# Layer 0's attention scores on column halves, with its last turns and layer 1's first norm in another order

## The chip, the cores and the metric

The kernel runs on one core of one Trainium2 chip. The metric is the device time of one execution in microseconds; a smaller time is better. Engines are named as in the profile: PE is TensorE (PEld its weight loads), DVE is VectorE, ACT is ScalarE, POOL is GpSimd, and SP is the engine that issues most DMAs.

## The reference, cut to what matters

Two transformer layers on x of 2 batches x 512 tokens x 512 features, all in float32. Each layer is attention and then a feed-forward, both on a normalised x that is scaled and shifted by columns of `mod`, and both added to x times a gate:

```
mod = silu(c) @ wmod                       # six rows of 512 per batch: shift, scale, gate, twice
h   = layernorm(x) * (1 + ca) + sa
x   = x + ga * attention(h)
h   = layernorm(x) * (1 + cb) + sb
x   = x + gb * ffn(h)
```

Layer 0's attention has 8 key heads, each with 4 query heads of size 128. A query at position i sees only the keys j with i - 128 < j <= i:

```
scores = einsum('bqhgd,bshd->bhgqs', qg, k) * sm_scale
allowed = (j <= i) & (j > i - SLIDING_WINDOW)          # SLIDING_WINDOW = 128
attn   = softmax(where(allowed, scores, neg))
out    = attn @ v ;  return out @ wo
```

So 128 consecutive queries see at most 256 consecutive keys: the first 64 of them see only the first 192 of these, and the last 64 only the last 192. Layer 0's feed-forward is a dense product with a bias and a weighted sum of 16 low-rank updates. Layer 1's attention has 128 heads with latent keys, and takes most of the time; the change does not touch it.

## The kernel before

**Layer 0's attention** (`attention0`, L662). A unit is one key head and one batch: 16 units, batch 0 and batch 1 of a head in turn. Each unit has four turns, one for each block of 128 queries (`qb`). The loop over n (L812) runs one turn at a time, and its order is written out by hand for PE, ACT, DVE and POOL (`manual_schedule`): each of these engines works through its instructions in the order of the program. In turn n the loop issues

1. `scores` of turn n: 4 products (one a head) into the PSUM tile `s`; DVE adds the mask `band` (L743) and takes the negated maximum (L749); ACT takes four exponentials (L753). The keys are 256 wide, in the first block of a unit (`qb` 0) 128 wide;
2. keys, values or queries of the next unit (`roped`, L685, and `values`, L707);
3. `normalised` of turn n: DVE's reciprocal (L762), POOL's product (L763);
4. `turned` of turn n-1: transposes on PE (L772), copied from PSUM to `pT` by ACT and DVE (L774);
5. `output` of turn n-2: the product with wo (L797), DVE's product with the gate (`ya`, L805), POOL's addition to x (L806);
6. `mix` of turn n-1: the product with the values (L783), copied to `oT` by DVE (L790);
7. what stands in `aside` (the modulation products, `mod_rows`, L101, in early turns) and in `steps[n]`.

The tile `s` has one buffer, taken anew in each turn. Products leave PE through PSUM tiles of the tag `mm`, four buffers in rotation (`pmm`), shared by queries, values, mix, output, and all of `finale`.

**The end of layer 0** (`finale`, L568). The last unit's turns are n = 60 to 63, with no queries left to compute; n = 64 and 65 finish mix and output. `finale` gives `steps`, what is done after turn n, and `rest`, what is done after the loop. In them stand layer 0's second norm `n0` (statistics by DVE, L160; `rows`: a square root on ACT, L168, a reciprocal and four scaled tiles `xn` on DVE, L173; `turn`: transposes on PE, L182, that leave as `hT` through ACT for even and DVE for odd blocks of features, L192 and L190) and the feed-forward `Ffn0`: `bias` (the bias times the gate), `add_bias` (POOL, L246), `low` (L251, the low-rank inputs of a batch) and `tile` (L264 and L268, one block of 128 tokens). Batch 0's attention is complete some turns before batch 1's, so its norm and its `low` are done beside the last turns.

**The start of layer 1** (`attention1`). Under a second hand-written order come the loads of the down-projections (L946) and of `Wq_up` and `Wk_up` (L950), whose halves ACT casts (L953, L954) and DVE subtracts (L955). Then, for each batch, `normalised` (the last function of `adaln_kernel`) and three down-projections (L971), whose results leave through DVE (L981) into a pool `psm1a` of three PSUM buffers. For batch 0 `normalised` transposes layer 1's first norm, `norm1`, and takes batch 1's statistics and rows; for batch 1 it transposes and spreads the gates (L140).

**The start of the kernel.** `silu_c` (L76) loads c for each layer on POOL's queue; SP's queue loads the modulation weights, x, the tables and layer 0's weights.

Of the kernel before, what the change touches and what calls it, by code (L numbers as in the profile page):

```python
# [10 lines left out]
F32 = mybir.dt.float32  # L11
# [7 lines left out]
P = 128  # L19
# [4 lines left out]
EPS = 1e-5  # L24

NKV, GRP, HD, WIN = 8, 4, 128, 128

NH, HD1, LAT, ROPE = 128, 4, 64, 64
SCALE1 = float(1.0 / np.sqrt(np.float32(HD1 + ROPE)))
# [13 lines left out]
def adaln_kernel(ctx: ExitStack, tc: tile.TileContext, A: dict, out: bass.AP):  # L43
# [161 lines left out]
    class Ffn0:  # L205
# [6 lines left out]
        def loads(self):  # L212
            self.wT = self.wmp.tile([P, KC, D], F32, tag="wmod", name="wT0", bufs=2)
            nc.sync.dma_start(out=self.wT, in_=A["L0_ffn_WT"].rearrange("(kc p) o -> p kc o", p=P))

            self.ab = self.wmp.tile([P, KC, D], F32, tag="wmod", name="abT0", bufs=2)
            nc.sync.dma_start(
                out=self.ab[:, :, : 2 * P], in_=A["L0_ffn_AT"].rearrange("(kc p) e -> p kc e", p=P)
            )
            for j in range(2):  # L220
                nc.sync.dma_start(
                    out=self.ab[:, 2 * j : 2 * j + 2, 2 * P :],
                    in_=A["L0_ffn_BT"][j * P : (j + 1) * P, :].rearrange("p (h o) -> p h o", h=2),
                )
            co = self.mid.tile([P, 2, 2], F32, tag="co", name="co0")
            for i, n in enumerate(("L0_ffn_coeffs", "L0_ffn_scales")):
                for j in range(2):
                    src = A[n][j * 8 : (j + 1) * 8].unsqueeze(1).to_broadcast([8, R]).unsqueeze(2)
                    nc.sync.dma_start(out=co[:, i, j : j + 1], in_=src)
            self.wrow = self.mid.tile([P, 2], F32, tag="wrow", name="wrow0")  # L230
            nc.vector.tensor_mul(self.wrow, co[:, 0, :], co[:, 1, :])

        def bias(self):

            row = self.ap.tile([P, D], F32, tag="t1", name="biasrow0")
            nc.sync.dma_start(out=row, in_=A["L0_ffn_bias"].unsqueeze(0).to_broadcast([P, D]))
            self.gb = [
                self.ap.tile([P, D], F32, tag="t2", name=f"gb{b}") for b in range(B)
            ]
            for b in range(B):  # L240
                nc.gpsimd.tensor_mul(self.gb[b], row, self.gate[b])
            self.xa = self.ap.tile([P, GRP, S], F32, tag="qT", name="xa")

        def add_bias(self, b):
# [280 lines left out]
    with ExitStack() as c01:  # L525
# [7 lines left out]
        with ExitStack() as c00:  # L533
# [34 lines left out]
            def finale(ap, pool):  # L568
# [44 lines left out]

        def normalised(b, pool):

            norm1.turn(b, range(KC), pool)
            if b == 0:
                for t in range(TB, NT):
                    norm1.stats(t)
                norm1.rows(1)  # L620
            else:
                spread_gates(1, (2, 5), grow[1], pool, gate)


# [3 lines left out]
def weights0(tc, A, ctx):  # L628
# [10 lines left out]
    def tables():  # L639

        rope = tab.tile([P, 4, S], F32, tag="rope", name="rope")
        nc.sync.dma_start(out=rope, in_=A["c_rope"])
        band = tab.tile([P, 2 * P], F32, tag="band", name="band")
        nc.sync.dma_start(out=band, in_=A["c_band"])
        return rope, band

# [15 lines left out]
def attention0(tc, small, hT, xs, ga, ident, tabs, groups, load_group, aside, finale):  # L662
# [11 lines left out]
    with ExitStack() as ctx:  # L674
# [4 lines left out]
        kTs, vs, qTs, oTs, sps, pes, pTs = ({} for _ in range(7))  # L679

        def roped(dst, wcols, b, tables, name):

# [47 lines left out]

        def scores(u, qb):

            k0, nk = window(qb)
            sp = pss.tile([P, GRP, 2 * P], F32, tag="s", name=f"s{u}_{qb}")
            for hh in range(GRP):
                nc.tensor.matmul(  # L736
                    sp[:, hh, :nk],
                    lhsT=qTs[u][:, hh, qb * P : (qb + 1) * P],
                    rhs=kTs[u][:, k0 * P : k0 * P + nk],
                    start=True,  # L740
                    stop=True,
                )
            nc.vector.tensor_add(  # L743
                sp[:, :, :nk],
                sp[:, :, :nk],
                band[:, 2 * P - nk :].unsqueeze(1).to_broadcast([P, GRP, nk]),
            )
            nm = small.tile([P, GRP], F32, tag="nm", name=f"nm{u}_{qb}")
            nc.vector.tensor_reduce(nm, sp[:, :, :nk], AX.X, ALU.max, negate=True)  # L749
            pe = ap.tile([P, GRP, 2 * P], F32, tag="p", name=f"p{u}_{qb}", bufs=3)  # L750
            rs = small.tile([P, GRP], F32, tag="rs", name=f"rs{u}_{qb}")
            for hh in range(GRP):
                nc.scalar.activation(  # L753
                    pe[:, hh, :nk], sp[:, hh, :nk], AF.Exp,
                    bias=nm[:, hh : hh + 1], accum_out=rs[:, hh : hh + 1],
                )
            pes[u, qb] = pe, rs
# [48 lines left out]
            nc.gpsimd.tensor_add(xs[t], xs[t], y)  # L806

        aside = aside(pmm)
        steps, rest = finale(ap, pmm)
        aside.pop(0)()  # L810
        with tc.manual_schedule(engines=FOUR):
            for n in range(-TB, NU * TB + 2):  # L812
# [725 lines left out]
def _constants():  # L1538
# [12 lines left out]
    band = np.where((j > i) & (j <= i + WIN), 0.0, -1e30).astype(np.float32)  # L1551

    r = np.arange(P) % 16
    lowq = (r // 4 % 2 == 1).astype(np.float32)
# [70 lines left out]
```

## Time and profile before

| | us |
|---|---|
| median of 3 runs | 2522.49 (2519.63 to 2522.56) |
| the profiled execution's own time | 2519.66 |
| its span, from first to last instruction | 2517.9 |
| PE busy in the span | 2453.7 (97%) |
| DVE busy | 1684.2 (67%) |
| ACT busy | 1401.9 (56%) |
| POOL busy | 1571.9 (62%) |

Layer 0's attention takes the span up to about 866 us, its feed-forward up to about 916, layer 1 the rest. A line of a timeline reads: start in us from the span's start, duration in us, engine, line of the kernel, operation, what is written <- what is read, shape in the array and of the operands, how many records; in brackets the idle time before it and what ended it. A product of f32 operands shows as two PE records. The durations of PE's records overlap, so the distance from start to start tells what one costs.

### The profile page before, as it was taken

What the parts mean: (1) busy time and instruction counts of PE and PEld (TensorE: products, weight loads), DVE (VectorE), ACT (ScalarE), POOL (GpSimd) and SP (SyncE); (2) the same over time, 40 slices, a digit from 0 to 9 for tenths busy, and PEclk for the clock granted to TensorE, in tenths of its full rate; (3) what the DMA queues carried; (4) which work ended last, traced back from release to release, by engine and by line L of the source; (5) the groups of instructions that cost most, each with busy time, mean ns of one, the idle gap of its engine ahead of it and who ended that gap; (6) DMA issues with size and microseconds to landing.
All of it is one profiled execution on the core that took longest, in us unless ns stands there. A gap on an engine that the chain in (4) does not pass through costs nothing.

```text
span 2517.9 us, 28439 instructions
## 1 busy us (share of the span) xinstructions
PE 2453.7 (97%) x10252; PEld 1146.2 (46%) x10252; DVE 1684.2 (67%) x2309; ACT 1401.9 (56%) x2086; POOL 1571.9 (62%) x1521
## 2 busy tenths in 40 slices
PE   8999999999999899999999999999999999999877
PEld 3555555555555444444443444444344444444333
DVE  4445555555555435787778777778778877788764
ACT  2212112121221215888888788888888878888650
POOL 1333333333334323888888888888888888888643
PEclk9999999999999999999999999999999999999978
DMA  6211101001000100000000000000100000110000
GB/s 240 88 49 60 42 5 38 26 20 40 17 1 7 29 15 26 26 26 26 26 26 17 29 27 26 26 18 26 30 26 26 18 25 26 30 29 21 17 9 34
DMA packets 68697, 81.32 MB, mean 32 GB/s; under 512 B 6989, under 2 KB 49772, under 8 KB 68428
## 3 DMA queue, kind: packets, MB, share of 16 engines
q1 hardware_dynamic: 68348, 79.35, 10.1%
q8 instruction: 81, 1.33, 0.2%
q14 instruction: 60, 0.49, 0.1%
q0 software_dynamic: 208, 0.16, 0.0%
HBM read 77.40 MB, written 2.10 MB: 32 GB/s over the span
## 4 chain that ended last, share of the span: by engine, by line
PE 95%; DVE 3%; ACT 1%; DMA 0%; issue 0%; POOL 0%; SPq 0%; DVEq 0%; ACTq 0%; POOLq 0%
PE s L1081 19%; PE psq L1014 18%; PE acc L1236 10%; PE ps_q L685 9%; PE pw L797 8%; PE s L1090 5%; PE s L736 4%; PE po L783 4%; PE psv L707 2%; PE ps_k L685 2%; PE pt L772 2%; PE psu L1033 2%; PE psm L1160 2%; PE psw L1292 1%; PE psf L499 1%; PE psf L264 1%
## 5 line engine op out<-in xcount | busy, mean ns | idle before, releaser
L1187 POOL TENSOR_TENSOR ss<-ss,row 128x512 f32<-128x512 f32 x504 | 634.5, 1287 | 42.8 <-ACT row L1172 42.8
L1100 ACT COPY ss<-s 128x1024 f32<-128x1024 f32 x512 | 505.4, 1015 | 179.2 <-PE s L1090 130.5
L1081 PE MATMUL s<-q,ckr 64*128 64x512 f32 x2048 | 554.5, 612 | 10.7 <-ACT ss L1100 10.7
L1190 ACT ACTIVATE ss<-ss 128x1024 f32<-128x1024 f32 x512 | 525.2, 1070 | 5.6 <-DVE ss L1402 4.5
L1014 PE MATMUL psq<-hT,wqr 128*128 128x512 f32 x1024 | 466.7, 598 | 0.0
L1090 PE MATMUL s<-qm,c 64*128 64x512 f32 x1024 | 419.7, 795 | 0.4 <-DVE c L1051 0.4
L753 ACT ACTIVATE p<-s,nm 128x256 f32<-128x256 f32 (+1 forms) x256 | 110.9, 445 | 489.6 <-DVE nm L749 480.8
L1107 DVE TENSOR_TENSOR mx<-s,mx 128x1024 f32<-128x1024 f32 x256 | 306.6, 1218 | 41.2 <-PE s L1090 40.1
L695 POOL TENSOR_TENSOR qT<-t_q,t_q 128x512 f32<-128x512 f32 x64 | 81.2, 1269 | 402.6 <-DVE t_q L694 402.6
L1181 POOL TENSOR_TENSOR ss<-ss,rowe 128x512 f32<-128x512 f32 x252 | 317.9, 1285 | 0.0
L1014 PEld LDWEIGHTS psq<-hT,wqr 128*128 128x128 f32 x1024 | 189.0, 189 | 242.3 <-issue 211.7
L1081 PEld LDWEIGHTS s<-q,ckr 64*128 64x128 f32 x2048 | 184.1, 186 | 215.8 <-ACT ss L1100 97.3
L1236 PE MATMUL acc<-ss,vp 128*32 128x512 f32 x2048 | 266.9, 614 | 0.0
L1107 DVE TENSOR_TENSOR mx<-s,ss 128x1024 f32<-128x1024 f32 x128 | 156.7, 1224 | 117.1 <-ACT row L1172 79.7
L797 PE MATMUL pw<-wo,oT 128*128 128x512 f32 x512 | 230.3, 592 | 0.0
L685 PE MATMUL ps_q<-hT,wq 128*128 128x512 f32 x512 | 230.1, 592 | 0.0
L1112 DVE STREAM_TRANSPOSE mx<-mx 128x1024 f32<-128x1024 f32 x128 | 158.6, 1239 | 2.3
L1118 DVE TENSOR_REDUCE m<-mx 128x32 f32<-128x1024 f32 x128 | 156.1, 1219 | 4.4
L1090 PEld LDWEIGHTS s<-qm,c 64*128 64x128 f32 x1024 | 104.6, 187 | 118.8 <-issue 114.6
L1150 POOL TENSOR_TENSOR st<-mh,own_block 128x512 fp32r<-128x512 f32 x64 | 67.0, 1047 | 142.9 <-DVE mh L1146 142.9
L1183 DVE TENSOR_TENSOR ss<-ss,psm 128x512 f32<-128x512 f32 x252 | 155.7, 679 | 0.0
L685 PEld LDWEIGHTS ps_q<-hT,wq 128*128 128x128 f32 x512 | 96.0, 190 | 102.3 <-issue 100.6
(208 smaller groups left out, 3089.5 us busy)
## 6 DMA issues: line engine op xcount, KB each, us to landing
wqr<-in_L_attn_Wq_rope_pairs SPq DMA_DIRECT2D x64, 512.0 KB
wmod<-in_L_wmod SPq DMA_DIRECT2D x12, 1024.0 KB
wq<-in_L_attn_wq SPq DMA_DIRECT2D x8, 1024.0 KB
wo<-in_L_attn_wo SPq DMA_DIRECT2D x8, 1024.0 KB
x<-in_L_attn_x SPq DMA_DIRECT2D x8, 256.0 KB
wk<-in_L_attn_wk SPq DMA_DIRECT2D x8, 256.0 KB
wv<-in_L_attn_wv SPq DMA_DIRECT2D x8, 256.0 KB
out<-yf SPq DMA_DIRECT2D x8, 256.0 KB
```

The costliest lines, as they stand in the source:

```text
L685: nc.tensor.matmul(ps, lhsT=wcols(kc), rhs=hT[b][:, kc, :], start=(kc == 0), stop=(kc == KC - 1))
L797: nc.tensor.matmul(ps, lhsT=oTs[u][:, hh, i * P : (i + 1) * P], rhs=groups[g]["o"][:, hh, :], start=(hh == 0), stop=(hh == GRP - 1),)
L1014: nc.tensor.matmul(ps, lhsT=wqs[t][:, kc, pair * P : (pair + 1) * P], rhs=hT[b][:, kc, :], start=(kc == 0), stop=(kc == KC - 1),)
L1081: nc.tensor.matmul(out[:, j, :], lhsT=whole[b]["kr"][r, bass.ts(i, P)], rhs=qs[t, p][r, :], start=True, stop=False,)
L1090: nc.tensor.matmul(out[:, j, :], lhsT=qkc[t // 2, 1][r, bass.ts(i, P)], rhs=qm[t, p][r, :], start=False, stop=True,)
L1100: nc.scalar.copy(ss[t, i, p], hold["s", t, i, p])
L1107: nc.vector.tensor_max(mx[t, p], hold["s", t, i, p], before)
L1112: nc.vector.transpose(m, m)
L1181: nc.gpsimd.tensor_sub(s, s, hold["r", t, 2])
L1187: nc.gpsimd.tensor_sub(s, s, hold["r", t, 2 * p + 1])
L1190: nc.scalar.activation(ss[t, i, p], ss[t, i, p], AF.Exp)
L1236: nc.tensor.matmul(accs[g, b][32 * h : 32 * (h + 1), :], lhsT=vps[t][:, kb, h, :], rhs=ss[t, kb, h // 2][:, h % 2, :], start=(s == 0 and k ...
```

## The change

- **Scores.** For `qb` above 0 each head's product is two: queries 0 to 63 of the block against keys 0 to 191 into output rows 0 to 63, queries 64 to 127 against keys 64 to 255 into rows 64 to 127. One PSUM tile `sp` is taken once and filled with -1e30 by DVE; the corners that no product writes keep that value, and `band` is 0 there. In block 0 the 128 keys now stand in the right half of the tile, with a third block of columns in `band` for them.
- **c first.** The loads of c go to SP's queue, ahead of the modulation weights.
- **The bias row** of feed-forward 0 gets a buffer of its own and is loaded with the other constants of the feed-forward (turn 20), not in turn 60.
- **The end of layer 0.** Statistics and rows of `n0`'s batch 0 come one turn later; a new list `filling` puts its four transposes, `add_bias` and the first `low` between output and mix of turn 63, and the second `low` between output and mix of turn 64; the last statistic and `tile(2)` change places in `rest`.
- **Layer 1's first norm.** `norm1`'s statistics and rows of batch 0 come between tiles 4 to 6 of the feed-forward, and its transposes between tiles 6 and 7; `normalised(0)` only takes batch 1's statistics and rows.

The diff, without the changes that only rename or copy:

```diff
@@ silu_c
-        nc.gpsimd.dma_start(out=c, in_=A[f"L{L}_cT"])
+        nc.sync.dma_start(out=c, in_=A[f"L{L}_cT"])
@@ Ffn0.loads, Ffn0.bias
+            self.row = self.mid.tile([P, D], F32, tag="biasrow", name="biasrow0")
+            nc.sync.dma_start(out=self.row, in_=A["L0_ffn_bias"].unsqueeze(0).to_broadcast([P, D]))
...
-            row = self.ap.tile([P, D], F32, tag="t1", name="biasrow0")
-            nc.sync.dma_start(out=row, in_=A["L0_ffn_bias"].unsqueeze(0).to_broadcast([P, D]))
@@ finale
                 for i in range(TB):
-                    steps[end + 2 + i] = [lambda i=i: n0.stats(i)]
-                    steps[end + 6 + i] = [lambda i=i: n0.stats(TB + i)]
+                    steps[end + 3 + i] = [lambda i=i: n0.stats(i)]
+                for i in range(TB - 1):
+                    steps.setdefault(end + 7 + i, []).append(lambda i=i: n0.stats(TB + i))
                 steps[end + 4].insert(0, f.bias)
-                steps[end + 5].append(lambda: n0.rows(0))
-                steps[end + 6].insert(0, lambda: n0.turn(0, (0, 1), pool))
-                steps[end + 7] = [
-                    lambda: n0.turn(0, (2, 3), pool), lambda: f.add_bias(0), lambda: f.low(0, 0)
-                ] + steps[end + 7]
-                steps[end + 8].insert(0, lambda: f.low(0, 1))
+                steps[end + 6].insert(1, lambda: n0.rows(0))
+
+                filling = {
+                    end + 7: [
+                        lambda: n0.turn(0, (0, 1), pool), lambda: n0.turn(0, (2, 3), pool),
+                        lambda: f.add_bias(0), lambda: f.low(0, 0),
+                    ],
+                    end + 8: [lambda: f.low(0, 1)],
+                }
                 rest = [
+                    lambda: n0.stats(NT - 1),
                     lambda: n0.rows(1),
                     lambda: f.tile(0),
                     lambda: f.tile(1),
+                    lambda: f.tile(2),
                     lambda: n0.turn(1, range(KC), pool),
                     lambda: f.add_bias(1),
-                    lambda: f.tile(2),
                     lambda: f.tile(3),
                     lambda: f.low(1, 0),
                     lambda: f.low(1, 1),
                 ]
-                for t in range(TB, NT):
-                    rest.append(lambda t=t: f.tile(t))
-                    rest.append(lambda t=t: norm1.stats(t - TB))
-                rest.append(lambda: norm1.rows(0))
-                return steps, rest
+                for i in range(TB):
+                    if i < 2:
+                        rest.append(lambda i=i: norm1.stats(i))
+                    rest.append(lambda i=i: f.tile(TB + i))
+                    if i == 1:
+                        rest.append(lambda: norm1.stats(2))
+                        rest.append(lambda: norm1.stats(3))
+                        rest.append(lambda: norm1.rows(0))
+                    if i == 2:
+                        rest.append(lambda: norm1.turn(0, range(KC), pool))
+                return steps, filling, rest
@@ normalised
-            norm1.turn(b, range(KC), pool)
-            if b == 0:
+            if b:
+                norm1.turn(b, range(KC), pool)
+            else:
@@ attention0
+        sp = pss.tile([P, GRP, 2 * P], F32, tag="s", name="scores")
+        nc.vector.memset(sp, NEVER)
@@ scores
             k0, nk = window(qb)
-            sp = pss.tile([P, GRP, 2 * P], F32, tag="s", name=f"s{u}_{qb}")
-            for hh in range(GRP):
+            o = 2 * P - nk
+            for hh in range(GRP) if qb == 0 else ():
                 nc.tensor.matmul(
-                    sp[:, hh, :nk],
-                    lhsT=qTs[u][:, hh, qb * P : (qb + 1) * P],
-                    rhs=kTs[u][:, k0 * P : k0 * P + nk],
+                    sp[:, hh, o:],
+                    lhsT=qTs[u][:, hh, :P],
+                    rhs=kTs[u][:, :P],
                     start=True,
                     stop=True,
                 )
+            for hh in range(GRP) if qb else ():
+                for h in range(2):
+                    lo, hi = h * H2, 2 * P - (1 - h) * H2
+                    nc.tensor.matmul(
+                        sp[h * H2 : (h + 1) * H2, hh, lo:hi],
+                        lhsT=qTs[u][:, hh, qb * P + h * H2 : qb * P + (h + 1) * H2],
+                        rhs=kTs[u][:, k0 * P + lo : k0 * P + hi],
+                        start=True,
+                        stop=True,
+                    )
             nc.vector.tensor_add(
-                sp[:, :, :nk],
-                sp[:, :, :nk],
-                band[:, 2 * P - nk :].unsqueeze(1).to_broadcast([P, GRP, nk]),
+                sp[:, :, o:],
+                sp[:, :, o:],
+                band[:, 0 if qb else 2 * P :][:, :nk].unsqueeze(1).to_broadcast([P, GRP, nk]),
             )
@@ the loop of attention0
                 if 0 <= n - 2:
                     output(*last)
+                for f in filling.get(n, ()):
+                    f()
                 if 0 <= n - 1 < NU * TB:
                     mix(*before)
@@ _constants
+    band = np.concatenate([band, band[:, P:]], axis=1)
+    band[:H2, 2 * P - H2 : 2 * P] = 0.0
+    band[H2:, :H2] = 0.0
```

More of the change, by code (lines that the diff above doesn't have):

```diff
@@ L26 @@
 NKV, GRP, HD, WIN = 8, 4, 128, 128
+H2 = P // 2
+NEVER = -1e30
 NH, HD1, LAT, ROPE = 128, 4, 64, 64
@@ L240, in bias @@
             for b in range(B):
-                nc.gpsimd.tensor_mul(self.gb[b], row, self.gate[b])
+                nc.gpsimd.tensor_mul(self.gb[b], self.row, self.gate[b])
             self.xa = self.ap.tile([P, GRP, S], F32, tag="qT", name="xa")
@@ L620, in normalised @@
                 norm1.rows(1)
-            else:
+            if b:
                 spread_gates(1, (2, 5), grow[1], pool, gate)
@@ L642, in tables @@
         nc.sync.dma_start(out=rope, in_=A["c_rope"])
-        band = tab.tile([P, 2 * P], F32, tag="band", name="band")
+        band = tab.tile([P, 3 * P], F32, tag="band", name="band")
         nc.sync.dma_start(out=band, in_=A["c_band"])
@@ L678, in attention0 @@
         pmm = ctx.enter_context(tc.tile_pool(name="psm0", bufs=4, space=PSUM, reuse_waits="tile"))
-        kTs, vs, qTs, oTs, sps, pes, pTs = ({} for _ in range(7))
+        kTs, vs, qTs, oTs, pes, pTs = ({} for _ in range(6))
+        sp = pss.tile([P, GRP, 2 * P], F32, tag="s", name="scores")
+        nc.vector.memset(sp, NEVER)
         def roped(dst, wcols, b, tables, name):
@@ L742, in scores @@
                 )
+            for hh in range(GRP) if qb else ():
[8 more added lines that the diff above has]
+                    )
             nc.vector.tensor_add(
-                sp[:, :, :nk],
-                sp[:, :, :nk],
-                band[:, 2 * P - nk :].unsqueeze(1).to_broadcast([P, GRP, nk]),
+                sp[:, :, o:],
+                sp[:, :, o:],
+                band[:, 0 if qb else 2 * P :][:, :nk].unsqueeze(1).to_broadcast([P, GRP, nk]),
             )
             nm = small.tile([P, GRP], F32, tag="nm", name=f"nm{u}_{qb}")
-            nc.vector.tensor_reduce(nm, sp[:, :, :nk], AX.X, ALU.max, negate=True)
+            nc.vector.tensor_reduce(nm, sp[:, :, o:], AX.X, ALU.max, negate=True)
             pe = ap.tile([P, GRP, 2 * P], F32, tag="p", name=f"p{u}_{qb}", bufs=3)
@@ L753, in scores @@
                 nc.scalar.activation(
-                    pe[:, hh, :nk], sp[:, hh, :nk], AF.Exp,
+                    pe[:, hh, :nk], sp[:, hh, o:], AF.Exp,
                     bias=nm[:, hh : hh + 1], accum_out=rs[:, hh : hh + 1],
@@ L808, in attention0 @@
         aside = aside(pmm)
-        steps, rest = finale(ap, pmm)
+        steps, filling, rest = finale(ap, pmm)
         aside.pop(0)()
@@ L1550, in _constants @@
     i, j = np.arange(P)[:, None], np.arange(2 * P)[None, :]
-    band = np.where((j > i) & (j <= i + WIN), 0.0, -1e30).astype(np.float32)
+    band = np.where((j > i) & (j <= i + WIN), 0.0, NEVER).astype(np.float32)
+    band = np.concatenate([band, band[:, P:]], axis=1)
+    band[:H2, 2 * P - H2 : 2 * P] = 0.0
+    band[H2:, :H2] = 0.0
     r = np.arange(P) % 16
```

## The prediction

> **What bounds the kernel now.** I read the chain that ended last, then the groups by line, then the stretches that the change touches as timelines. The chain's shares by engine:
>
> ```profile
> PE 95%; DVE 3%; ACT 1%; DMA 0%; issue 0%; POOL 0%; SPq 0%; DVEq 0%; ACTq 0%; POOLq 0%
> ```
>
> TensorE (PE) is the path. In the stage table it is busy for 747.3 of the 748 us between 60 and 808 us (layer 0's attention), for 50.5 of 58 between 808 and 866 (its end), and for 31.2 of 34 between 916 and 950 (the start of layer 1). So in attention an edit counts only by PE time; at the two seams by the PE gaps.
>
> **Part 1, scores on column halves.** PE timeline, one score step (L736) with its neighbours, 128*128 in the array throughout:
>
> ```profile
> 324.03 1.88 PE L783 MATMUL po<-pT,v 128*128 128x512 f32 x4
> 325.75 1.89 PE L736 MATMUL s<-kT,qT 128*128 128x256 f32 x8
> 327.47 3.73 PE L707 MATMUL psv<-wv,hT 128*128 128x128 f32 x32
> ```
>
> Read the starts: four 512-column records take 1.72 us, 0.429 each; eight 256-column ones 1.726, 0.216 each (four heads, two records for each f32 product). That is 0.8 ns a column and 2.5 ns more; 192 columns give 0.1625. Entering and leaving cost nothing. The new step issues 16 records of 64 output rows by 192 columns, half on rows 0-63 of the output, half on 64-127. Do two such halves run together, and is the change of shape free? No 64-column record exists here. The nearest row is the modulation product (L101), two neighbouring groups of 32:
>
> ```profile
> 113.10 1.88 PE L783 MATMUL po<-pT,v 128*128 128x512 f32 x4
> 114.91 3.63 PE L101 MATMUL psr<-wmod,sc 128*32 128x512 f32 x16
> 118.47 1.99 PE L736 MATMUL s<-kT,qT 128*128 128x256 f32 x8
> 120.30 0.94 PE L707 MATMUL psv<-wv,hT 128*128 128x128 f32 x7
> ```
>
> 16 records of 512 columns last about 8x0.429 = 3.43, so pairs do overlap fully. But L783 is through at 113.10+4x0.429 = 114.82, and 114.82 to 120.30 is 5.48, against 3.43+1.73 = 5.16 of streaming: 0.32 is lost by going in and out. Single records split it: on entry 0.092 before the first weight load starts and 0.026 for that load; on leaving 0.098 and 0.106. The Trainium skill, "TensorEngine Tiling (Array Packing)", Key Properties, has the rule that speaks against this change: going from one tiling mode to another drains the engine. Its "TensorE: Matmul & The Clock Gate", LDWEIGHTS, prices a load at columns/1.2 ns; the trace's 26 (32 columns) and 106 ns (128) agree, and 64 columns, which no row has, come to an estimated 53. So a new wide step is 8x0.1625 = 1.300 + 0.092+0.053 + 0.098+0.107 = 1.65, not 1.30: **-0.077 a step, 48 wide steps (16 units x 3): -3.7 us**. Without the drain rule it would be -0.426x48 = -20.5. Bounds: -20.5 (no price for the change of shape) and +59 (halves one after the other: 16x0.1625+0.35 = 2.95 a step). I take -3.7, since L101 measures both. DVE, ACT and POOL do the same work on the same shapes. The one-off fill of the score tile (128x1024 on DVE, nearest row the 1.23 us band addition) falls behind layer 0's first norm, where PE streams K and Q from 25 us on without waiting for DVE; uncovered it costs 1.2.
>
> **Part 2, the start.** The two loads of c leave POOL's queue and go ahead of the modulation weights on SP. The first products do wait for c (7.77 us), but their second half is released by
>
> ```profile
> 8.84 0.18 PEld L101 LDWEIGHTS psr<-wmod,sc 128*32 128x32 f32 x3 [0.89 <-DMA wmod<-in_L_wmod]
> ```
>
> so c early gains nothing. SP's issues here take 0.45 to 0.50 each, so wmod and x queue up to 0.9 later; between 0 and +0.9, as the DMA engines are full from 3 us on, I take **+0.6**. ffn 0's bias row moves to SP's issues at 40 us, long before use.
>
> **Part 3, the end of layer 0** (loop turns 60 to 65: no queries are left to cover the softmax). The costliest wait now is 5.47 us of PE in turn 62:
>
> ```profile
> 834.78 3.78 PE L783 MATMUL po<-pT,v 128*128 128x512 f32 x4 [5.47 <-ACT pT L774]
> ...
> 862.47 3.60 PE L797 MATMUL pw<-wo,oT 128*128 128x512 f32 x8
> ```
>
> DVE and ACT say why: the norm's rows (4 xn, 1.92 us, after a statistic that waits 1.12 for POOL) stand before the band addition, and the square root costs ACT a table load before the exponentials.
>
> ```profile
> 828.44 1.23 DVE L743 TENSOR_TENSOR s<-s,band 128x1024 f32<-128x1024 f32 x1
> 831.02 1.28 ACT L753 ACT_TABLE_LOAD   x1 [4.66 <-DVE nm L749]
> 834.13 0.60 ACT L774 COPY pT<-pt 128x512 f32<-128x512 f32 x1
> 834.28 0.18 DVE L762 RECIPROCAL rs<-rs 128x4 f32<-128x4 f32 x1 [3.36 <-ACT p L753]
> 834.96 0.68 DVE L805 TENSOR_TENSOR ya<-pw,g 128x512 f32<-128x512 f32 x1
> ```
>
> From band addition to pT copy's end is 6.3, to ya's end 7.2. The change moves this block one turn later and puts four transposes and the first `low` between output and mix. On the old clock the new order runs so. Turn 62: add at 824.9, no table load, mix at 829.9, a wait of 0.9. Then DVE: oT copy to 832.5, stats and rows to 835.85 (old: 825.12 to 828.44), band addition there, ya done at 843.05. PE in turn 63: scores, transposes, output to 837.6, three of the four new transposes to 838.9; the fourth needs the `mm` buffer (four in rotation) of the same turn's output, held by ya until 843.05. So what is moved in as filling waits for the same DVE queue: **the stall goes, but 4.2 us come back one turn later**. Then `low` to 847.0, mix to 848.7. Turn 64 goes through output and the second `low` to 856.5 and mix to 858.3; output 63 now follows its mix at once and waits 0.95 for the oT copy (that `low` used to hide it): end 862.65, old 862.47+3.43 = 865.90, **-3.2**. The clock takes part of it. The granted clock fell after these windows (columns: length, PE busy, PEld, DVE, ACT, POOL, clock, DMA):
>
> ```profile
> 829.50:832.80 3.30, 0.00 (x0) 0.00 (x0) 1.39 (x2) 1.76 (x4) 0.00 (x0) 1.00 0.00 0
> 914.80:918.20 3.40, 1.08 (x3) 0.19 (x1) 1.77 (x5) 0.30 (x1) 1.65 (x3) 1.00 0.82 212
> ```
>
> and stayed at a half for 6.8 us each time. "TensorE: Matmul & The Clock Gate", Part 1, has it fall after one idle window of about 3.4 us; here 1.08 of 3.40 busy sufficed. Of 4.2 idle us, one 3.4-window catches over 2.3 in nearly every phase, so it falls again. By the page's rule alone, a full window, it would mostly not, and I would leave out the next term: some 3 us of work at half speed, +1.6. **Sum -1.6**; ends -3.2 and 0.
>
> **Part 4, layer 1's first norm.** Today its batch 0 is transposed after the last feed-forward tile:
>
> ```profile
> 918.70 4.75 PE L182 MATMUL pst<-ident,xn 128*128 128x128 f32 x16 [2.82 <-DVE xn L173]
> 923.25 4.55 PE L971 MATMUL pscq<-hT,L_attn_Wq_down 128*128 128x512 f32 x8
> 938.70 3.70 PE L971 MATMUL pscq<-hT,L_attn_Wq_down 128*128 128x512 f32 x8
> ```
>
> Call U the end of the last tile's streaming (915.72). Batch 1's L971 starts at U+22.98. The new order puts the 16 transposes (1.75, as at 876.2) between tiles 6 and 7: rows come from DVE while tile 6 (5.15 us) streams, so nothing waits, and batch 0's L971 can start at U and end at U+10.3. But DVE then works through the two `up` differences (L955), which wait for Wq_up's load and ACT's casts, four statistics and batch 1's rows before it empties the first L971 buffer (the old run: 924.22 to 929.91, 5.7 us). L955 ends at 922.2 now (U+6.5), of which about 1.5 goes with the xn work ahead of it and with Wk_rope's issues, likely free sooner as the wider band shifts the feed-forward weights by 512 B: U+5. So the first emptying starts at U+10.7, the others 2 and 4 us later, and with three buffers batch 1's four transposes wait 1.1, 1.5 and 1.6: done at U+16.3, gate rows, L971 at U+18.6. Gain 22.98-18.6-1.75 = 2.6; without the shift 1.7. These waits make another nearly empty window; transposes there did not restore the clock before (918.2 to 921.6). I take +1.8: **-0.8**, ends -2.6 and +1.
>
> **Sum.** -3.7+0.6-1.6-0.8 = **-5.5 us**. The profiled execution took 2519.66 (span 2517.9 and 1.8 around it), which gives 2514.2. The median of three is 2522.49, 2.8 above it; two of three runs lie there. Taken off the median: **2517.0**. A measurement here tells about 0.2% (5.0 us) from no change.
>
> **Rivals.** (a) **The seams return nothing**: part 3's and 4's waits and clock falls cost all they save (DVE is late by the same work, wherever it stands). For: the dependence of every filler on DVE. Against: 865.90 against 862.65. -3.7+0.6+0.5: about 2520, chance 0.22. (b) **More than I grant**: the clock stays up at both seams (-8.9, 2513.5; chance 0.07), for which the free phase of the windows speaks, or the change of shape is free (-22, 2500; 0.04), against which L101 speaks. (c) **Slower**: the weight loads are not hidden behind passes as short as 0.16. Eight loads of 53 ns show in each wide step: 2.07 in place of 1.73, +0.35x48 = 16.7, less 1.8: about 2537. Against: L707 hides 128-column loads behind 128-column passes at 0.11 a record. For: there all of the array is one group. It decides from 1.87 us a step, (1.8+5.0)/48 above today's. Chance 0.12.
>
> **Chances and range.** My forecast 0.55, itself 2512 to 2522: its middle lies near the 0.2% bound, so 0.33 faster and 0.22 the same. With (a) 0.20 same and 0.02 slower, (b) 0.11 faster, (c) 0.12 slower: faster 0.44, same 0.42, slower 0.14. The range 2509 to 2526 leaves out the free change of shape and most of (c).
>
> **What would show it.** Wide L736 steps 1.65 us start to start of the neighbours (1.30: drain wrong; 2.07 or 2.95: loads or halves exposed). In turn 62 a PE wait below 1.5; in turn 63 one near 4 us ahead of the fourth transpose, released by DVE ya; a wait before output 63. No wait before layer 1's first L971, but waits for `fq`, `ckv`, `ckr` ahead of batch 1's transposes. A wrong price of the shape change moves the sum most: 0.1 us is 4.8.

## The result and the profile after

The changed kernel takes **2512.44 us** (median of 5 runs, 2509.96 to 2514.69); the kernel before, run beside it, 2522.49 (median of 5, 2517.6 to 2522.95). The ratio is **0.9967, 95% interval 0.9954 to 0.998**: faster by 0.33%. The forecast was 2517.0 (2509 to 2526): sign and range held, and the gain in the median, 10.05, is nearly twice the 5.5 of the sum. The excess is less sure than it looks: the means differ by 8.7, and in the 19 and 22 runs beside the experiments the kernel before has medians of 2519.6 and 2520.53, against which the gain is 7 to 8. The profiled execution took 2511.97, its span fell from 2517.9 to 2510.2.

How the -7.7 of the span is spread over the stages shows that the sum came near for the wrong reasons. The borders are starts of PE records in the two traces: first query product, first scores of layer 0 (turn 0), scores of turn 60, first feed-forward product `psf`, first scores of layer 1's attention, end.

| stage | before | after | difference | predicted |
|---|---|---|---|---|
| start to first query product | 25.21 | 29.55 | **+4.34** | +0.6 |
| on to the scores of turn 0 | 27.86 | 29.75 | +1.89 | 0 |
| turns 0 to 60 (45 wide steps) | 755.11 | 750.21 | **-4.90** | -3.5 |
| turn 60 to `psf` (3 wide steps) | 57.72 | 56.61 | -1.11 | -1.8 |
| `psf` to layer 1's scores | 95.53 | 90.54 | **-4.99** | -0.8 |
| rest of layer 1 | 1556.5 | 1553.5 | -2.9 | 0 |

A stage is read from one traced execution of each kernel. PE's granted clock falls to a half for 3.4 to 17.1 us at a time, and which work such a window covers differs from trace to trace; a stage can move by 1 to 2 us by that alone.

PE is still the path. The chain that ended last, shares by engine:

```profile
PE 94%; DVE 4%; ACT 1%; DMA 0%; issue 0%; SPq 0%; POOL 0%; DVEq 0%; ACTq 0%
```

**Scores.** PE timeline of the changed kernel, the step that answers to the one at 324 us of before:

```profile
327.71 1.88 PE L812 MATMUL po<-pT,v 128*128 128x512 f32 x4
329.52 1.52 PE L765 MATMUL scores<-kT,qT 128*64 128x192 f32 x16
330.97 3.84 PE L725 MATMUL psv<-wv,hT 128*128 128x128 f32 x32
```

L812 streams until 327.71+4x0.429 = 329.43. The values product streams from 331.08 (the next record group starts at 334.65, less 32 records at 0.1116). Between lies 1.65 us, the price that was worked out: the sixteen records run in eight pairs, and the shape change costs 0.35.

Where modulation products stand ahead of the scores, the step gains more:

```profile
118.51 1.88 PE L812 MATMUL po<-pT,v 128*128 128x512 f32 x4
120.32 3.63 PE L103 MATMUL psr<-wmod,sc 128*32 128x512 f32 x16
123.88 1.52 PE L765 MATMUL scores<-kT,qT 128*64 128x192 f32 x16
125.33 1.94 PE L725 MATMUL psv<-wv,hT 128*128 128x128 f32 x15
```

From L812's end (118.51+1.72 = 120.23) to the streaming of the values (125.44: the next product starts at 129.00, less 3.57 as above) it takes 5.21, before 5.48: 0.27 less, not 0.077. The array had already left 128*128 for the modulation product, and now comes back once for both: lost beside 3.43+1.30 of streaming are 0.48, against 0.32+0.35 for two separate departures.

**End of layer 0.** PE in turns 62 to 65, and what ACT and DVE do ahead of the fourth transpose:

```profile
830.91 1.98 PE L812 MATMUL po<-pT,v 128*128 128x512 f32 x4 [0.66 <-ACT pT L803]
...
838.64 1.47 PE L184 MATMUL pst<-ident,xn 128*128 128x128 f32 x12
843.87 1.12 PE L184 MATMUL pst<-ident,xn 128*128 128x128 f32 x4 [3.75 <-ACT hT L194]
844.78 5.67 PE L253 MATMUL psxa<-hT,abT 128*128 128x512 f32 x8
...
862.58 3.70 PE L826 MATMUL pw<-wo,oT 128*128 128x512 f32 x8 [0.78 <-DVE oT L819]
```

```profile
839.43 1.28 ACT L782 ACT_TABLE_LOAD   x1 [4.66 <-DVE nm L778]
...
843.00 1.48 ACT L194 ACTIVATE hT<-pst,mod,mod 128x512 f32<-128x512 f32 x2
```

```profile
843.36 0.68 DVE L834 TENSOR_TENSOR ya<-pw,g 128x512 f32<-128x512 f32 x1
```

The 5.47 us wait is 0.66; 3.75 came back one turn later, and the clock fell from 842.1 to 848.9, so that the first `low` (L253) took 5.67 and not 3.60.

**Layer 1's first norm.** PE from the first down-projection on:

```profile
917.68 3.60 PE L1002 MATMUL pscq<-hT,L_attn_Wq_down 128*128 128x512 f32 x8
...
929.13 0.66 PE L184 MATMUL pst<-ident,xn 128*128 128x128 f32 x4 [0.99 <-DVE fq L1012]
929.83 0.47 PE L1064 MATMUL psu<-chq,upg 128*128 128x512 f32 x1
930.51 0.50 PE L1064 MATMUL psu<-clq,upg 128*128 128x512 f32 x1 [0.21 <-DVE clq L1015]
930.84 1.02 PE L1045 MATMUL psq<-hT,wqr 128*128 128x512 f32 x2
931.70 0.60 PE L184 MATMUL pst<-ident,xn 128*128 128x128 f32 x4
932.14 1.02 PE L1045 MATMUL psq<-hT,wqr 128*128 128x512 f32 x2
...
936.74 3.70 PE L1002 MATMUL pscq<-hT,L_attn_Wq_down 128*128 128x512 f32 x8
```

Nothing waits before the first L1002, and batch 1's transposes wait 0.99 for `fq`. After that PE is idle for only 0.21: between the transposes stand an up-projection of layer 1's batch 0 (L1064) and query products (L1045), work that has to be done anyway. The query products all came later before (from 949.34).

**Start.** ACT before, then ACT and DVE after. L168 and L170 are the square root of batch 0's norm, L109 and L111 the copy of the modulation rows, L122 the modulation columns:

```profile
12.96 1.28 ACT L168 ACT_TABLE_LOAD   x1 [4.95 <-DVE mv L161]
...
14.88 0.58 ACT L109 COPY rows<-psr 64x512 f32<-64x512 f32 x1 [0.33 <-PE psr L101]
```

```profile
14.79 0.58 ACT L111 COPY rows<-psr 64x512 f32<-64x512 f32 x1 [11.62 <-PE psr L103]
16.39 1.28 ACT L170 ACT_TABLE_LOAD   x1 [1.02 <-DVE mv L163]
```

```profile
12.72 0.66 DVE L162 BATCH_NORM_STATS2 bn<-x 128x6 f32<-128x512 f32 x1
15.97 0.24 DVE L122 TENSOR_SCALAR mod<-psm 128x8 f32<-128x8 f32 x2 [2.60 <-PE psm L119]
16.13 0.17 DVE L163 BATCH_NORM_AGGREGATE mv<-bn 128x2 f32<-128x6 f32 x1
...
18.40 1.89 DVE L175 TENSOR_SCALAR xn<-x,mv,rstd 128x512 f32<-128x512 f32 x4
```

x itself is 0.8 late (first statistic at 10.30, before 9.51). But the last 0.17 us of batch 0's statistics stand behind the modulation columns in DVE's order, and the square root behind the copy of the modulation rows in ACT's. So the first `xn` comes at 18.40; before it came at 15.17. After PE's wait for it, its clock falls (columns as in the forecast's rows):

```profile
16.10:19.50 3.40, 0.52 (x4) 0.38 (x5) 3.40 (x13) 1.58 (x2) 0.00 (x0) 1.00 1.06 327
```

From 19.5 to 22.9 it stands at a half, and the transposes there start 0.213 apart in place of 0.109.

### The profile page after: what moved, and what is told of

The parts are those of the page before. It is cut to its first block, busy times and chain, and to the rows that moved or that the text cites. A ratio compares the mean times of both kernels' runs of the same rounds, so it can differ in the third digit from the quotient of the medians.

```text
span 2510.2 us, 29183 instructions
## 1 busy us (share of the span) xinstructions
PE 2446.2 (97%) x10636; PEld 1119.3 (45%) x10636; DVE 1684.2 (67%) x2310; ACT 1402.3 (56%) x2086; POOL 1573.2 (63%) x1519
## 4 chain that ended last, share of the span: by engine, by line
PE 94%; DVE 4%; ACT 1%; DMA 0%; issue 0%; SPq 0%; POOL 0%; DVEq 0%; ACTq 0%
PE s L1112 19%; PE psq L1045 18%; PE acc L1267 10%; PE ps_q L703 9%; PE pw L826 8%; PE s L1121 5%; PE po L812 4%; PE scores L765 3%; PE psv L725 2%; PE ps_k L703 2%; PE pt L801 2%; PE psu L1064 2%; PE psm L1191 2%; PE psw L1323 1%; PE psf L501 1%; PE psf L266 1%
## 5 line engine op out<-in xcount | busy, mean ns | idle before, releaser
L1045 PE MATMUL psq<-hT,wqr 128*128 128x512 f32 x1024 | 467.2, 598 | 0.0
L782 ACT ACTIVATE p<-scores,nm 128x256 f32<-128x256 f32 (+1 forms) x256 | 111.2, 446 | 482.4 <-DVE nm L778 473.4
L1045 PEld LDWEIGHTS psq<-hT,wqr 128*128 128x128 f32 x1024 | 188.9, 189 | 241.0 <-issue 210.4
```

The source lines that it names most:

```text
L1045: nc.tensor.matmul(ps, lhsT=wqs[t][:, kc, pair * P : (pair + 1) * P], rhs=hT[b][:, kc, :], start=(kc == 0), stop=(kc == KC - 1),)
```

## The experiments

Two questions were open. First, why the start lost 4.3: because SP's queue brings x later (the forecast's reason), or because the order of DVE and ACT is another one. Second, why layer 1's first norm gained 5.0 and not 0.8. Medians are compared with runs of the kernel before on the same chip, which differed by up to 9 us among themselves; so most of the reading is by stages, from the one trace of each kernel. That trace is not always of a middling run: those of "end of layer 0" and "no filling" are the slowest of their kernels. All stages in us, cut as above:

| kernel | to turn 0 | 0 to 60 | 60 to `psf` | `psf` to layer 1's scores | rest |
|---|---|---|---|---|---|
| before | 53.07 | 755.11 | 57.72 | 95.53 | 1556.5 |
| after | 59.30 | 750.21 | 56.61 | 90.54 | 1553.5 |
| c on POOL | 54.43 | 749.55 | 55.83 | 90.48 | 1553.7 |
| c on SP, start ordered by hand | 53.28 | 747.98 | 56.89 | 92.59 | 1555.4 |
| before + c on SP | 59.81 | 754.04 | 57.20 | 96.87 | 1558.8 |
| before + scores | 53.60 | 750.04 | 57.74 | 95.99 | 1553.6 |
| before + layer 1's first norm | 54.59 | 755.26 | 57.81 | 93.16 | 1555.7 |
| before + end of layer 0 | 55.66 | 754.19 | 57.58 | 95.07 | 1556.2 |
| c on POOL, no filling | 54.83 | 750.42 | 56.73 | 97.23 | 1553.9 |
| c on POOL, rows later | 54.98 | 750.17 | 51.69 | 90.51 | 1555.1 |
| two shape changes a step | 60.07 | 774.98 | 55.60 | 91.78 | 1558.8 |

### c back on POOL's queue

```diff
-        nc.sync.dma_start(out=c, in_=A[f"L{L}_cT"])
+        nc.gpsimd.dma_start(out=c, in_=A[f"L{L}_cT"])
```

> The changed kernel with only the loads of c put back on POOL's queue. Theory A (what c first costs is an order: with c early, the builder puts the copy of the modulation rows ahead of the square root on ACT, and the modulation columns ahead of batch 0's last statistic on DVE): both queues return to their old order, the first query record starts near 25.3 us instead of 29.55, and the time is 4 to 6 us less than the changed kernel's 2512.4, about 2507. Rival B (only SP's issues are late, by 0.8): the first query record near 28.7, the time about 2511.6.

Measured: 2507.27, ratio 0.9946 (0.9934 to 0.9959). The first query product starts at 25.73 (after: 29.55), turn 0's scores at 54.43. The rest of the change keeps its gains. Moving c alone costs the change 3.8 to the first query product and 4.9 to turn 0, and the median shows it too (2507.27 against 2512.44, though these were not run side by side).

### c on SP's queue, with the start's order written by hand

The queue stays as in the change; only the order of DVE, ACT and PE at the start is fixed. `root` and `scaled` are the two halves of `rows`.

```diff
-                mod_columns(0, w, mod_rows(0, w, scs[0], pmm, wmp), pmm)
+                c0.enter_context(tc.manual_schedule(engines=FOUR))
                 norm = Norm(0, 0, 1, mid)
-                for b in range(B):
-                    norm.batch(b, pmm)
+                for t in range(TB):
+                    norm.stats(t)
+                norm.root(0)
+                for t in range(TB, NT - 1):
+                    norm.stats(t)
+                norm.scaled(0)
+                mod_columns(0, w, mod_rows(0, w, scs[0], pmm, wmp), pmm)
+                norm.stats(NT - 1)
+                norm.turn(0, range(KC), pmm)
+                norm.rows(1)
+                norm.turn(1, range(KC), pmm)
```

> The changed kernel with c still first on SP, but the start's order on DVE and ACT written out by hand as the kernel before had it (statistics and square root of batch 0 before the modulation columns). Theory A: batch 0's first scaled tile starts near 16.0 instead of 18.4 us, the first query record near 26 to 27 instead of 29.55, the time about 3 us under the changed kernel's, 2509. Rival B (the late SP queue): nothing moves, first query record near 29.5, 2512.

Measured: 2508.55, ratio 0.9957 (0.9945 to 0.997). ACT and DVE of this kernel:

```profile
13.76 1.28 ACT L174 ACT_TABLE_LOAD   x1 [10.71 <-DVE mv L163]
```

```profile
16.16 1.91 DVE L183 TENSOR_SCALAR xn<-x,mv,rstd 128x512 f32<-128x512 f32 x4
```

Here x is as late as in the changed kernel (first statistic at 10.38), and yet the square root comes at 13.76 and the first query product at 26.32. So the order accounts for 3.2 (29.55 against 26.32): 2.2 is the later first `xn` (18.40 against 16.16), and 1.0 comes behind it, where the changed kernel had the clock at a half and this one did not. The queue keeps the rest, 0.6 to 1.1: with c on POOL the first query product of the changed kernel starts at 25.73 here, and at 25.30 and 25.20 in the two later kernels with the same start. The forecast's 0.6 is the low end.

### The kernel before, with c on SP's queue alone

```diff
-        nc.gpsimd.dma_start(out=c, in_=A[f"L{L}_cT"])
+        nc.sync.dma_start(out=c, in_=A[f"L{L}_cT"])
```

> The kernel before with only the loads of c moved to SP, ahead of the weights. Theory A: the first query record goes from 25.2 to about 29.5 us, the time 4 to 6 us up, about 2527. Rival B and the prediction's own step (+0.6): 25.8 to 26, about 2523.

Measured: 2528.15, ratio 1.0028 (1.0018 to 1.0038): alone this one line makes the kernel slower. The first query product is at 30.88, and the same reversal of order is in its trace (square root at 17.55, behind the copy of the modulation rows at 15.95); here the clock was at a half for 6.8 us, from 18.3. The wider band and the fill of the score tile are absent here, so they are not the cause.

### The kernel before, with the scores on halves alone

The edit is the part "Scores" of the diff above: `sp`, `scores` and `band`.

> The kernel before with only the scores on column halves. With the change of shape priced as predicted (1.65 for 1.73 us a step): 3.7 us less, about 2518.8. Rival, the whole gain of 10 us comes from here, since the stage from the first scores to the last unit lost 4.9 us in the two traces: 4.9 to 8 us less, 2515 to 2517.5. Rival, the change of shape is free: 20 us less.

Measured: 2512.91 (2509.95 to 2519.22), ratio 0.9976 (0.9967 to 0.9986): 6 to 7 us less, and so nearer to the first rival than to the 3.7. Turns 0 to 60 take 750.04, 5.07 less than before; layer 1's scores start 4.1 earlier. Most of this kernel's gain is thus the part's own. The further 2.9 of its profiled span lie in the rest of layer 1, where nothing was edited.

### The kernel before, with layer 1's first norm alone

The edit is the part "Layer 1's first norm": `norm1` in `rest`, and `normalised`.

> The kernel before with only layer 1's first norm moved into the feed-forward. Theory C (the waits of batch 1's transposes are filled: the builder's order puts layer 1's first query products between them, so the clock stays up): from the first feed-forward product to layer 1's first scores 5.0 us less than before's 95.5, the time about 2515. Rival, the prediction's own step (waits of 1 to 1.6 us that stay empty, and a fall of the clock): 0.8 us less.

Measured: 2519.3, ratio 0.999 (0.9979 to 1.0001), not clear of no change. The stage is 93.16, -2.4 where -5 was expected. Its PE timeline has the query products between the transposes as well, but:

```profile
931.59 0.66 PE L182 MATMUL pst<-ident,xn 128*128 128x128 f32 x4 [1.91 <-DVE fq L988]
```

The wait for `fq` is 0.92 longer than in the changed kernel, and the clock fell for 3.4 us after it, which costs 1.7. Without these two the part would give the -5.0 (2.4+0.9+1.7). The same order can thus gain 2.4 or 5.0. It is not alone in this: with c on SP and the start ordered by hand the clock also fell here, from 923.2 for 3.4 us, and the stage took 92.59.

### The kernel before, with the end of layer 0 alone

The edit is the parts "The end of layer 0" and "The bias row".

> The kernel before with only the end of layer 0 reordered and the bias row loaded early. As predicted: a wait near 0.9 us in turn 62, about 4 us ahead of the fourth transpose in turn 63, a fall of the clock after it; from turn 60's scores to the first feed-forward product 1.1 to 1.6 us less than before's 57.7, the time 1 to 2 us less. Rival, the reorder removes the wait for good: 6 to 8 us less.

Measured: 2518.01, ratio 0.999 (0.9981 to 0.9999), which agrees with the 1 to 2 us that were expected. The waits came as expected, 0.80 and 3.63. In the trace, of the slowest of the ten runs, the stage takes 57.58, only 0.14 less than before; the changed kernel is 0.97 below it. Of that 0.23 is the three wide steps. Most of the remainder is the clock's phase: here its half-speed window began at 843.9, in the changed kernel at 842.1, both for 6.8 us, and PE stood idle for the first 0.84 of the one and 1.77 of the other. PE loses nothing at half speed while it is idle, so the first had 0.9 us more of work to do at half speed, some 0.5 us dearer.

### No query products between the transposes

With c on POOL's queue, as the first experiment. The pool of layer 1's query buffers is opened ahead of two others, so that it lies in other PSUM banks; in the trace its products then start only behind batch 1's down-projections, at 947.0.

```diff
+        pX = ctx.enter_context(tc.tile_pool(name="pX1", bufs=3, space=PSUM, reuse_waits="tile"))
         pS = ctx.enter_context(tc.tile_pool(name="pS1", bufs=1, space=PSUM, reuse_waits="tile"))
         pA = ctx.enter_context(tc.tile_pool(name="pA1", bufs=1, space=PSUM, reuse_waits="tile"))
-        pX = ctx.enter_context(tc.tile_pool(name="pX1", bufs=3, space=PSUM, reuse_waits="tile"))
```

> As the run with c on POOL's queue, but the PSUM pools of layer 1 are opened in another order, so that the query products' buffers lie on those of the down-projections, and no query product can stand between batch 1's transposes. Theory C: those waits are empty again, together 3 to 4 us, and the clock falls; from the first feed-forward product to layer 1's first scores 94 to 95 us in place of 90.5, the time 3 to 5 us over that run's 2507.3. Rival, the filling pays nothing since the products are only done earlier: no change there.

Measured: 2511.45, ratio 0.9961 (0.9948 to 0.9974). Its PE timeline:

```profile
925.32 0.65 PE L184 MATMUL pst<-ident,xn 128*128 128x128 f32 x4 [1.31 <-DVE fq L1012]
927.29 1.12 PE L184 MATMUL pst<-ident,xn 128*128 128x128 f32 x4 [1.32 <-DVE ckv L1012]
928.62 1.97 PE L184 MATMUL pst<-ident,xn 128*128 128x128 f32 x8 [0.21 <-ACT hT L194]
930.61 3.78 PE L142 MATMUL psg<-grow,ident 64*128 64x512 f32 x4
934.32 5.05 PE L1002 MATMUL pscq<-hT,L_attn_Wq_down 128*128 128x512 f32 x8
```

This is what the forecast had drawn: waits for `fq`, `ckv` and (almost none) `ckr`, and a clock at half speed, here for 10.2 us. The stage is 97.23, 6.75 above the first experiment's and 1.7 above the kernel before; the rest of layer 1 takes the same as in the first experiment (1553.9 against 1553.7). The trace is of the slowest of five runs, and the medians, not run side by side, differ by 4.2. So the filling, with the clock that it kept up, is worth 4 to 7 us, and in this trace the move of the norm without it has lost. In this trace 1.4 is the clock, still at a half under batch 1's first product (5.05 for 3.70).

### n0's rows behind the band addition

Also with c on POOL's queue. In turn 63 the reciprocal and the four scaled tiles of `n0` come after the band addition and the maximum; the square root stays.

```diff
-                steps[end + 6].insert(1, lambda: n0.rows(0))
+                steps[end + 6].insert(1, lambda: n0.root(0))
+
+                beside = {end + 7: [lambda: n0.scaled(0)]}
@@ the loop of attention0
                     scores(u, qb)
+                for f in beside.get(n, ()):
+                    f()
```

> As the run with c on POOL's queue, but in turn 63 the norm's reciprocal and scaled tiles come behind the band addition and the maximum on DVE instead of ahead of them (the square root stays where it is). If the 3.75 us wait ahead of the fourth transpose is the queue on DVE, it falls to between 1.2 and 2 us, the clock need not fall, and the time is 2 to 4 us under 2507.3, about 2504. Rival, ACT's table load and exponentials set it whatever stands on DVE: no change.

Measured: 2505.01, ratio 0.9943 (0.9931 to 0.9956).

```profile
837.07 0.66 PE L192 MATMUL pst<-ident,xn 128*128 128x128 f32 x4 [1.24 <-ACT hT L202]
837.57 3.60 PE L261 MATMUL psxa<-hT,abT 128*128 128x512 f32 x8
```

The wait ahead of the fourth transpose falls from the first experiment's 3.76 to 1.24, and the clock stays up, where it fell there for 3.4 us. The stage takes 51.69, 4.1 less than in the first experiment: 2.5 of the wait and 1.7 of the clock. It confirms what the forecast said of this wait: what is moved in as filling waits for the same queues, and the rows stand ahead of the exponentials. Its median is the lowest of the study, and each of its runs (2504.46 to 2508.12) is below each of the changed kernel's (from 2509.96), though it also has c on POOL. Its interval overlaps with the first experiment's; in the trace the rest of layer 1 gave 1.4 back.

### Two shape changes in a step

The changed kernel, with heads 0 and 2 on halves and heads 1 and 3 whole, in turn. The band keeps its mask in the corners.

```diff
-                for h in range(2):
+                for h in range(2) if hh % 2 == 0 else ():
...
+                if hh % 2:
+                    nc.tensor.matmul(
+                        sp[:, hh, :],
+                        lhsT=qTs[u][:, hh, qb * P : (qb + 1) * P],
+                        rhs=kTs[u][:, k0 * P : (k0 + 2) * P],
+                        start=True,
+                        stop=True,
+                    )
```

> The changed kernel, but in each wide step only heads 0 and 2 are in column halves, and heads 1 and 3 whole, in turn, so that the array changes shape twice in a step. If going in and out costs 0.35 us each time: 2x(0.325+0.35)+4x0.216 = 2.21 us a step against the changed kernel's 1.65, 27 us more in all, about 2539. If the change of shape is free or paid once: 1.51 to 1.86 a step, 2506 to 2523.

Measured: 2544.25, ratio 1.0092 (1.0062 to 1.0121).

```profile
336.40 1.88 PE L820 MATMUL po<-pT,v 128*128 128x512 f32 x4
338.21 0.55 PE L765 MATMUL scores<-kT,qT 128*64 128x192 f32 x4
338.69 0.70 PE L773 MATMUL scores<-kT,qT 128*128 128x256 f32 x2
339.32 0.55 PE L765 MATMUL scores<-kT,qT 128*64 128x192 f32 x4
339.79 0.70 PE L773 MATMUL scores<-kT,qT 128*128 128x256 f32 x2
340.33 3.73 PE L725 MATMUL psv<-wv,hT 128*128 128x128 f32 x32
```

From 336.40+1.72 = 338.12 to the start of the values' streaming at 340.33 (343.90, the next product, less 3.57) it takes 2.21. That is 0.65 for four half records in pairs, twice, 0.86 for four whole ones, and 2x0.35 = 0.70. The whole trace agrees: turns 16 to 60 take 561.79, 0.562 more a wide step than in the changed kernel, and 2.21-1.65 is 0.56. The price of the shape change holds per change, and a kernel that changes shape with each head loses the gain.

## Why the prediction was right, and where it was not

**Scores, -3.7: right, slightly small.** The step is 1.65 as worked out. From turn 16 to turn 60, where no modulation products are left, 33 wide steps gained 2.58 (545.84 to 543.26), 0.078 each against the forecast's 0.077. The further 1.4 of turns 0 to 60 lie in turns 0 to 16. Some 0.2 of it is the clock, at a half behind turn 0 for 4.5 us in place of 5.0. The rest fits the neighbours: of the 12 wide steps there, three have a modulation product right ahead and three the transposes of its rows (L117, 64*128); at 0.19 more each, read at one of them, they make 1.1. The forecast read its price off a modulation product with scores behind it, and did not ask what the neighbours' shape means: there the array changes shape anyway. The free shape change and the unhidden weight loads (rival c) are both excluded by the step.

**Start, +0.6: the step that failed.** "So c early gains nothing" was right, the queue's 0.6 was right or somewhat small (0.6 to 1.1), and the fill of the score tile was covered as said. What was left out is that the order of the engines at the start is not written by hand. It is made when the program is built, and with c earlier the modulation's followers stood ahead of the norm's. The instructions are the same, and their order cost +3.2 to the first query product, 1.0 of it with the fall of the clock. The +1.9 on the way to turn 0 is the half-speed window on the spreading of the gates (L142, 6.49 in place of 4.59). The edit need not have to do with it: the same products take 6.13 and 7.19 in the two kernels that leave the start alone (layer 1's norm, end of layer 0), and 3.70 with c on SP and the start ordered by hand, where the clock did not fall there.

**End of layer 0, -1.6: mechanism right, the clock's term too small.** Without its three wide steps the stage gave -0.9 (and in the trace of the part alone -0.1). Waits of 0.66, 3.75 and 0.78 stand for the forecast's 0.9, 4.2 and 0.95. The releaser was named wrongly: the fourth transpose followed ACT's `hT` of the first transposes, whose end at about 843.8 came just ahead of its start, not DVE's `ya`, which ended at 844.04; both stand behind the same exponentials. The term for the clock, +1.6, was some 2.5: from 843.87 to 848.9 PE worked at half speed, 5.0 us for 2.5 us of work.

**Layer 1's first norm, -0.8: the other step that failed.** The wait for `fq` is 0.99 (forecast 1.1), and `up`'s second difference ends at U+5.0, as taken. (It was U+5.9 with the norm alone and U+6.2 with two shape changes a step, which has the wider band too; so whether the shift by 512 B did it stays open.) Batch 1's L1002 starts at U+19.06, forecast U+18.6. But the terms "1.5 and 1.6" of further waits were counted as empty time, and "+1.8" was put in for the clock. The order between two hand-written stretches is again made at build, and it puts layer 1's products into the gaps. They are useful work. The stage's -5.0 is +1.74 for the sixteen transposes between tiles 6 and 7, -3.92 for batch 1's first L1002 (U+22.98 to U+19.06), and -2.81 for what is left from there to layer 1's scores (22.73 to 19.92), since the products in the gaps are already done; the +1.8 did not come. That the clock stayed up is in part luck: with the same products in the gaps it fell in two other kernels (stages of 93.16 and 92.59). The seventh experiment, without them, gives the forecast's picture, and a loss of 1.7.

**The sum.** The start's excess of 5.6 and the norm's excess gain of 4.2 nearly cancel; scores and end add -0.7. So at layer 1's first scores the trace is at -4.8, close to the forecast's -5.5, by errors of both signs: that is luck. The -2.9 in the rest of layer 1 were not foreseen. No edit touches that stage, and it varies from 1553.5 to 1558.8 over the kernels here, with 50 to 64 us at half clock after 2300 us. From before to after these fall from 56.9 to 53.6 us, which can account for at most 1.7 of the 2.9. Rival (a), that the seams return nothing, is refuted for layer 1's by the -5.0; for the end of layer 0 it was nearly true, with -0.9 in one trace and -0.1 in the other. Of rival (b) one half came true, the clock at layer 1's seam, with the luck just named. The rest's share in the median is not settled: what decides where these late windows fall was not isolated.

## What to carry to other kernels

An edit that only changes when a load arrives can change an order that is made at build, on engines that the load never touches: compare the order of each engine before pricing it, and write by hand an order that matters. A gap on the engine that sets the time is priced only when one has asked what else could stand in it. When pricing a change of array shape, look at the shape of the neighbours: two departures from the plain shape next to each other cost less than two apart (0.48 against 0.67 here).

## What the runs showed of the hardware

**How idle a window must be for the clock to fall.** In each trace all falls and rises of the granted clock lie on one grid of 3.413 us: in the changed kernel it falls at 19.5, 53.6 and 842.1, which is 10 and 231 steps apart. Four windows of that grid, columns as in the forecast's rows: of the changed kernel, of the kernel before, of that with the rows later, and of that with two shape changes a step.

```profile
838.70:842.10 3.40, 1.42 (x13) 1.18 (x11) 0.63 (x1) 2.66 (x8) 0.00 (x0) 1.00 0.00 0
```

```profile
47.79:51.20 3.41, 2.65 (x6) 1.23 (x7) 2.66 (x4) 1.17 (x2) 0.63 (x1) 1.00 0.02 2
```

```profile
834.40:837.80 3.40, 2.16 (x18) 1.80 (x17) 2.07 (x5) 3.29 (x11) 1.56 (x1) 1.00 0.00 0
```

```profile
951.12:954.53 3.41, 1.56 (x4) 0.38 (x2) 2.97 (x8) 0.30 (x1) 0.00 (x0) 1.00 0.00 0
```

After the first two the clock fell, after the last two it did not. "TensorE: Matmul & The Clock Gate", Part 1, speaks of an idle window; here windows in which PE was busy for 1.42 and even 2.65 us sufficed. No bound on PE's busy time alone fits these windows: one of 2.65 was followed by a fall, one of 1.56 was not. They differ in the kind of work. PE's work in the second was all spreading of gates, 64*128 in the array; in the third it was nearly all transposes; in the fourth it was all products of 128*128. Whether work on part of the array counts for less was not tested. How long the clock then stays down, 3.4, 6.8 or 10.2 us at the start and the seams, these runs do not explain.

**The shape change** has a price of 0.35 us in and out at 64 columns, in two kernels with one and two changes a step; and 192-column records in halves run in pairs at 0.16 us with their weight loads hidden.
